# A mixture-of-experts block: three first-layer block products split once more into seven, summed in place; the first half of the slots rotated by pairs of tiles

## The chip, the cores and the metric

The kernel is one program on one core of a Trainium2 chip. The metric is the device time of one execution in microseconds (us); the figure used is the median over the runs. The engines are named as in the profile: PE (TensorE matmul; PEld its weight loads), DVE (VectorE), ACT (ScalarE), POOL (GpSimd) and SP (SyncE, which only issues DMAs here).

## The reference, cut to what matters

```
x: (4, 1024, 512) fp32, E = 8 experts, 2 per token, hidden width 2048, all fp32
z      = rotate(filter(x))               # per token, four blocks of 128 mixed by a 4x4 matrix
scores = softmax(z @ gate_w.T);  top 2 experts of each token, gates normalised
disp   = tokens sorted into 8 experts x 1024 slots
h      = relu(disp @ fc1_w.T + fc1_b)    # per expert 1024 x 512 -> 1024 x 2048
eo     = h @ fc2_w + fc2_b               # per expert 1024 x 2048 -> 1024 x 512
out    = x + sum over the two experts of gate * eo
```

The filter's gain is the same at every frequency of a channel, so filter and rotation together are one 4x4 mixing matrix M per channel.

## The kernel before, in words

A prologue of some 45 us chooses the experts, sorts the tokens into slots and gathers the first expert's rows. After it one stream runs to the end. It goes over k = 0 to 31; k is the pair (expert e, hidden group g), with four hidden groups of 512 to an expert, so e, g = divmod(k, 4).

Both layers are done by blocks with seven products in place of eight (the Winograd form of Strassen's scheme). In the first layer the blocks are halves of the hidden group, of the 512 input columns and of the 1024 slots; a product has 256 hidden rows x 256 inputs x 512 slots, two row halves m by two contraction halves c, that is four matmuls of 128x128x512. The left factors are blocks of w1 and their sums s0 to s3, made on POOL by `left1` (L131). The right factors are blocks xa, xc, xb of the rotated input and their sums x0 to x3, made on POOL once per expert (`Slots.factors`). `layer1` (L780) issues the seven products in 14 units, one per row half; a unit is what the generator does between two `yield`s. ACT (L792) or DVE (L805, L821, L832) takes each product out of PSUM, adding the bias, or another product, and the relu. The four results h11, h21, h22, r12 then give four sums of 128x1024 on DVE, s1 to s4 (`chain`, L770), the left factors of the second layer.

The second layer (`second_layers`, L959) does the same with w2: for each k two column pairs of seven products, each four matmuls of 128x128x256 (`product2`, L757), 14 units again. DVE adds each product into v tiles or the accumulators; POOL makes the sums t0 to t3 of w2.

The order is written out by hand: the last loop takes one unit of the first layer, then one of the second, in turn; the second is some three units and one k behind. After each unit `turn()` (L740) issues one piece of `background` and one of `fetches`. Background holds DVE and ACT work that has no fixed place: `chain`, the turning and rotating of the next expert's rows (`Slots.steps`, L692: 32x32 transposes of a 128x512 square, then four weighted sums, L723), and the weighted stores of finished rows (L630). Fetches are indirect DMAs of POOL: quarters of the next expert's rows (L670), choices (L611), output rows (L587). Every engine works its own list in order, and semaphores tie the lists together.

k = 0 has no sums ready and uses `layer1_plain` (L836): all eight block products, for the first 512 slots, then the second 512. Before it `rotated(0)` (L887) transposes four tiles of 128 rows on PE and forms the rotated blocks by weighted sums of 512 columns.

PSUM has eight banks of 128x512: one for `ps_x`, four for `ps_1` (two tiles of two banks), three for `ps_2`.

## Time and profile before

| what | value |
|---|---|
| time, median of 3 runs | 1624.74 us (1624.31 to 1626.83) |
| profiled execution, own time | 1616.91 us |
| its span, first to last instruction | 1615.1 us |
| mean granted PE clock | 0.990 |
| busy: PE, PEld, DVE, ACT, POOL | 1581.1, 1043.0, 910.4, 290.3, 891.6 us |
| one k in the steady part | 48.2 us |

A row of a group of instructions reads: source line, engine, operation, names written and read, shapes, count, then busy us in total and mean ns of one, then the idle time of the engine before them and who ended it. The profile records an fp32 matmul as two instructions, so a product of four matmuls is eight records. Durations of neighbouring records on PE overlap; the pace is read from the starts in the chain of waits.

### The profile page before, as it was taken

The numbers are of one execution on the slowest core, as the hardware profiler recorded it, in microseconds if no ns is written. First come the engines' busy times: TensorE is split into PE (matmuls) and PEld (weight loads), VectorE is DVE, ScalarE is ACT, GpSimd is POOL, SyncE is SP. The second block draws the span as 40 slices with busy tenths as digits, with TensorE's granted clock in tenths as the row PEclk, the third lists the DMA queues.
The fourth block names the chain that finished last, engine by engine and source line by source line (L and its number), as shares of the span: only waits on it lengthen the run. The fifth ranks groups of instructions, "written<-read, shape, count | busy, mean of one in ns | idle before, by whom it ended". The sixth has DMA issues, their size and how long they took to land.

```text
span 1615.1 us, 14666 instructions
## 1 busy us (share of the span) xinstructions
PE 1581.1 (98%) x5631; PEld 1043.0 (65%) x5631; DVE 910.4 (56%) x1292; ACT 290.3 (18%) x417; POOL 891.6 (55%) x745
## 2 busy tenths in 40 slices
PE   6899999999999999999999999999999999999997
PEld 3456666666666666666666666666666666666666
DVE  6536744476555654567455774457744576454336
ACT  3121111221112211122111221122111221111110
POOL 1676265853568445783367725586266844544305
PEclk8799999999999999999999999999999999999999
DMA  7542103311222113320133210331122311230003
GB/s 315 191 139 70 53 28 117 114 61 52 98 91 78 54 52 111 124 85 1 52 130 115 76 53 0 142 112 66 53 82 68 111 56 53 100 114 17 36 27 103
DMA packets 47998, 137.31 MB, mean 85 GB/s; under 512 B 9334, under 2 KB 9590, under 8 KB 42808
## 3 DMA queue, kind: packets, MB, share of 16 engines
q1 hardware_dynamic: 22800, 75.54, 12.8%
q0 software_dynamic: 20736, 52.32, 9.9%
q10 hardware_dynamic: 4392, 8.52, 1.4%
q8 instruction: 44, 0.72, 0.2%
q14 instruction: 26, 0.21, 0.0%
HBM read 119.77 MB, written 25.23 MB: 90 GB/s over the span
## 4 chain that ended last, share of the span: by engine, by line
PE 95%; DMA 1%; DVE 1%; POOL 1%; issue 1%; SPq 0%; POOLq 0%; ACT 0%; DVEq 0%; ACTq 0%
PE a L761 27%; PE a L748 26%; PE b L761 20%; PE b L748 20%; PE p L859 2%; DMA xb<-in_xt_dram 1%; POOL rows L587 1%; DMA rows<-in_x_dram,slot_tok 0%; POOL out_dram L635 0%; DVE A L457 0%; DMA rows<-out_dram,slot_tok 0%; PE xps L713 0%; SPq L182 0%; DVE B L444 0%; DVE xa L723 0%
## 5 line engine op out<-in xcount | busy, mean ns | idle before, releaser
L792 ACT ACTIVATE u<-a,b_sb 128x512 f32<-128x512 f32 x186 | 127.7, 686 | 793.0 <-PE a L748 793.0
L670 POOL DMA_INDIRECT xq<-in_xq_dram,quarter x224 | 232.4, 1037 | 62.0 <-issue 59.9
L761 PEld LDWEIGHTS a<-t,hs 128*128 128x128 f32 x1024 | 194.6, 190 | 79.4 <-issue 59.3
L761 PE MATMUL a<-t,hs 128*128 128x256 f32 x1024 | 241.9, 379 | 0.0
L748 PE MATMUL a<-x,s 128*128 128x512 f32 x496 | 233.1, 592 | 0.0
L136 POOL TENSOR_TENSOR s<-w 128x512 f32<-128x512 f32 x31 | 39.3, 1268 | 218.1 <-PE b L748 218.0
L139 POOL TENSOR_TENSOR s<-w,s 128x512 f32<-128x512 f32 x31 | 40.8, 1316 | 202.6 <-PE b L748 202.5
L748 PEld LDWEIGHTS a<-x,s 128*128 128x128 f32 x496 | 94.2, 190 | 65.7 <-issue 59.3
L761 PEld LDWEIGHTS b<-w,h 128*128 128x128 f32 x512 | 97.2, 190 | 42.1 <-issue 20.8
L761 PEld LDWEIGHTS a<-t,h 128*128 128x128 f32 x512 | 97.1, 190 | 40.6 <-issue 24.6
L761 PE MATMUL b<-w,h 128*128 128x256 f32 x512 | 121.1, 379 | 2.1 <-DVE acc L1051 2.1
L761 PEld LDWEIGHTS a<-w,h 128*128 128x128 f32 x512 | 97.3, 190 | 39.7 <-issue 29.7
L761 PE MATMUL a<-t,h 128*128 128x256 f32 x512 | 121.1, 379 | 0.8 <-DVE v L1025 0.8
L761 PEld LDWEIGHTS b<-t,hs 128*128 128x128 f32 x504 | 95.8, 190 | 39.5 <-issue 23.2
L761 PEld LDWEIGHTS b<-w,hs 128*128 128x128 f32 x504 | 95.8, 190 | 39.0 <-issue 27.5
L761 PE MATMUL a<-w,h 128*128 128x256 f32 x512 | 120.9, 379 | 0.0
L761 PE MATMUL b<-t,hs 128*128 128x256 f32 x504 | 119.1, 379 | 0.0
L761 PE MATMUL b<-w,hs 128*128 128x256 f32 x504 | 119.1, 379 | 0.0
L748 PE MATMUL a<-xa,w 128*128 128x512 f32 x248 | 116.6, 592 | 0.8 <-ACT u L792 0.8
L748 PE MATMUL b<-xa,w 128*128 128x512 f32 x248 | 116.5, 592 | 0.0
L748 PE MATMUL a<-x,w 128*128 128x512 f32 x248 | 116.5, 592 | 0.0
L748 PE MATMUL b<-x,s 128*128 128x512 f32 x248 | 116.5, 592 | 0.0
(183 smaller groups left out, 2158.4 us busy)
## 6 DMA issues: line engine op xcount, KB each, us to landing
w<-in_w_dram SPq DMA_DIRECT2D x64, 1024.0 KB, 7.9
xb<-in_xt_dram SPq DMA_DIRECT2D x8, 1024.0 KB, 12.2
out_dram<-in_x_dram ACTq DMA_DIRECT2D x1, 8192.0 KB
xq<-in_xq_dram,quarter POOLq DMA_INDIRECT x224, 2.5
b<-in_b_dram POOLq DMA_DIRECT2D x8, 256.0 KB, 3.7
c<-choice,slot_cho POOLq DMA_INDIRECT x64, 2.5
rows<-out_dram,slot_tok POOLq DMA_INDIRECT x64, 6.4
out_dram<-rows,slot_add POOLq DMA_INDIRECT x64, 2.8
```

What stands on the lines that cost most here:

```text
L136: lambda: G.tensor_tensor(s[0], w[:, 1, 0], w[:, 1, 1], ALU.add),
L139: lambda: G.tensor_tensor(s[3], w[:, 0, 1], s[1], ALU.subtract),
L587: nc.gpsimd.indirect_dma_start(out=t, out_offset=None, in_=src, in_offset=bass.IndirectOffsetOnAxis(ap=slot_tok[:, s : s + 1], axis=0),)
L670: nc.gpsimd.indirect_dma_start(out=self.xg[half][st][:, q * P : (q + 1) * P], out_offset=None, in_=xq, in_offset=bass.IndirectOffsetOnAxis ...
L748: nc.tensor.matmul(out[:, m], lhsT=factors[0][n][:, c, m * P : (m + 1) * P], rhs=factors[1][n][:, c, :], start=first and c == 0, stop=c == ...
L761: nc.tensor.matmul(out[m] if isinstance(out, list) else out[:, m], lhsT=factors[0][n][:, c, (st0 + m) * P : (st0 + m + 1) * P], rhs=factor ...
L792: nc.scalar.activation(to[:, m], a[:, m], func, bias=bias[:, m : m + 1])
L859: nc.tensor.matmul(ps[n][:, m], lhsT=w[:, block, i // 2, i % 2, m * P : (m + 1) * P], rhs=x.of(half, i), start=i == 0, stop=i == NJ - 1,)
```

## The change

Of the first layer's seven products, 1, 3 and 2 are done by seven products of their own blocks: 128 hidden rows x 128 inputs x 256 slots each, one matmul of 256 columns instead of a share of 512-column ones. Their left factors are made per k by `left_sub` (eight POOL sums), their right factors once per expert by `right_sub` (twelve DVE sums). Class `Within` issues them in four steps, one, two, three, four; each product goes into half of a PSUM bank, in which later products accumulate, and DVE adds the bank's state at each step straight into h11, h21 or r12 in SBUF. Products 0, 5, 6 and 4 stay whole and come first (units 0 to 7); the split ones take units 8 to 13. h tiles come from a list of eleven free tiles. `ps_x` goes to `ps_1`, now five single banks, and the squares of the next expert's rows are turned into SBUF (`sqp`) instead of PSUM. POOL's sums for the next k move from units 7, 8, 9, 13 to 9, 10, 11, 13, the second half's quarter gathers from unit 6 of g = 1 to unit 10, its turning from unit 5 of g = 2 to unit 7. `turn` issues up to two pieces of background after a unit, by the table `PACE`, and at most one where g = 0.

At the start the first half's transposes are laid out so that two tiles of rows fill two banks; the weighted sums and the products of k = 0 then go over 256 slots at a time, first the first pair.

```diff
+    def left_sub(k, w, s4):
+
+        G = nc.gpsimd
+        both = wsum.tile([P, 2, 4, P], F32, tag="sub13", name=f"sub13_{k}")
+        one = wsum.tile([P, 1, 4, P], F32, tag="sub2", name=f"sub2_{k}")
+        factors, steps = {}, []
+        for t, block, names in ((both, w[:, :, 1], (1, 3)), (one, s4.unsqueeze(1), (2,))):
+
+            def b(m, c, block=block):
+                return block[:, :, c, m * P : (m + 1) * P]
+
+            def q(i, t=t):
+                return t[:, :, i]
+
+            steps += [
+                lambda b=b, q=q: G.tensor_tensor(q(0), b(1, 0), b(1, 1), ALU.add),
+                lambda b=b, q=q: G.tensor_tensor(q(1), q(0), b(0, 0), ALU.subtract),
+                lambda b=b, q=q: G.tensor_tensor(q(2), b(0, 0), b(1, 0), ALU.subtract),
+                lambda b=b, q=q: G.tensor_tensor(q(3), b(0, 1), q(1), ALU.subtract),
+            ]
+            for n, name in enumerate(names):
+                order = (b(0, 0), b(0, 1), q(3), b(1, 1), q(0), q(1), q(2))
+                factors[name] = [f[:, n] for f in order]
+        return factors, steps
+
+    def right_sub(pool, e, right):
+
+        factors, steps = {}, []
+        for n in (1, 3, 2):
+            t = pool.tile([P, 4, HS], F32, tag=f"xsub{n}", name=f"xsub{n}_{e}")
+
+            def b(c, h, block=right[n]):
+                return block[:, c, h * HS : (h + 1) * HS]
+
+            steps += [
+                lambda b=b, t=t: V.tensor_tensor(t[:, 0], b(0, 1), b(0, 0), ALU.subtract),
+                lambda b=b, t=t: V.tensor_tensor(t[:, 1], b(1, 1), t[:, 0], ALU.subtract),
+                lambda b=b, t=t: V.tensor_tensor(t[:, 2], b(1, 1), b(0, 1), ALU.subtract),
+                lambda b=b, t=t: V.tensor_tensor(t[:, 3], b(1, 0), t[:, 1], ALU.subtract),
+            ]
+            factors[n] = [b(0, 0), b(1, 0), b(1, 1), t[:, 3], t[:, 0], t[:, 1], t[:, 2]]
+        return factors, steps
...
-    hp = ctx.enter_context(tc.tile_pool(name="hp", bufs=2))
-    up = ctx.enter_context(tc.tile_pool(name="up", bufs=2))
-    rp2 = ctx.enter_context(tc.tile_pool(name="rp2", bufs=1))
+    hp = ctx.enter_context(tc.tile_pool(name="hp", bufs=1))
+    sqp = ctx.enter_context(tc.tile_pool(name="sqp", bufs=2))
...
-    ps_x = ctx.enter_context(tc.tile_pool(name="ps_x", bufs=1, space=PSUM))
-    ps_1 = ctx.enter_context(tc.tile_pool(name="ps_1", bufs=2, space=PSUM))
+    ps_1 = ctx.enter_context(tc.tile_pool(name="ps_1", bufs=5, space=PSUM))
...
+    def bank1(name):
+        return ps_1.tile([P, HALF], F32, tag="p1", name=name)
+
+    unused = [hp.tile([P, 2, HALF], F32, name=f"hidden{i}") for i in range(11)]
...
-                bank[j] = self.bank(half, j, ps_x, "xps")
+                bank[j] = self.bank(half, j, sqp, "sq")
...
-    def turn():
-        if background:
-            background.pop(0)()
+    def turn(n=1):
+        for _ in range(n):
+            if background:
+                background.pop(0)()
...
+        if st0 + 2 == PER and 1 in tiles:
+            unused.append(factors[0][n])
...
+    class Within:
+        def __init__(self, to, left, right, name):
+            self.to, self.left, self.right = to, left, right
+            self.bank = bank1(name)
+            self.a, self.b = self.bank[:, :HS], self.bank[:, HS:]
+        def times(self, out, n, first=False):
+            nc.tensor.matmul(
+                out,
+                lhsT=self.left[n],
+                rhs=self.right[n],
+                start=first,
+                stop=True,
+                skip_group_check=True,
+            )
+        def add(self, m, h, out):
+            to = self.to[:, m, h * HS : (h + 1) * HS]
+            V.tensor_tensor(to, out, to, ALU.add)
+        def one(self):
+            self.times(self.a, 0, True)
+            self.times(self.b, 1)
+        def one_added(self):
+            self.add(0, 0, self.a)
+            self.add(0, 0, self.b)
+        def two(self, c, first):
+            self.c = c
+            self.times(self.a, 5)
+            self.times(c, 4, first)
+        def two_added(self):
+            self.add(0, 1, self.a)
+        def three(self):
+            self.times(self.a, 6)
+        def three_added(self):
+            self.add(1, 1, self.a)
+            self.add(1, 1, self.c)
+        def four(self):
+            self.times(self.a, 3)
+            self.times(self.c, 2)
+        def four_added(self):
+            self.add(1, 0, self.a)
+            self.add(0, 1, self.c)
...
+        taken = []
+        for n, bias in ((0, lo), (5, lo), (6, hi)):
+            to = unused.pop(0)
+            taken.append(to)
+            for m in range(2):
+                half(a[m], m, n, n == 0)
+                nc.scalar.activation(to[:, m], a[m], AF.Identity, bias=bias[:, m : m + 1])
+                yield
+        h11, r12, h21 = taken
+        h22 = unused.pop(0)
+        for m in range(2):
+            b = bank1(f"b{m}_{k}")
+            half(b, m, 4, True)
+            V.tensor_tensor(r12[:, m], b, r12[:, m], ALU.add)
+            V.tensor_tensor(h22[:, m], b, h21[:, m], ALU.add)
+            if m == 1:
+                relu(h22)
+            yield
+        p1, p3 = (Within(h, *(f[n] for f in subs), f"w{n}_{k}") for n, h in ((1, h11), (3, h21)))
+        p1.one()
+        p3.one()
+        p1.one_added()
+        p3.one_added()
+        yield
+        c = bank1(f"c_{k}")
+        p1.two(c[:, :HS], True)
+        p3.two(c[:, HS:], False)
+        p1.two_added()
+        p3.two_added()
+        yield
+        p1.three()
+        p3.three()
+        p2 = Within(r12, *(f[2] for f in subs), f"w2_{k}")
+        p2.one()
+        p1.three_added()
+        p3.three_added()
+        p2.one_added()
+        yield
+        p1.four()
+        p3.four()
+        p2.two(bank1(f"c2_{k}")[:, :HS], True)
+        p1.four_added()
+        relu(h11)
+        p2.two_added()
+        p3.four_added()
+        relu(h21)
+        yield
+        p2.three()
+        p2.three_added()
+        yield
+        p2.four()
+        p2.four_added()
+        s1, s2, s3, s4 = (unused.pop(0) for _ in range(4))
         hidden[k] = [h11, h21, s4, h22, s1, s2, s3]
+        chain(h11, h21, h22, s1, s2, s3, s4, r12)
+        yield
...
+        def rotated_by_pairs():
+            t = banks(0)
+            for st in range(PER):
+                for j in range(NJ):
+                    at = (j % 2 * 2 + st % 2) * P
+                    nc.tensor.transpose(
+                        t[st // 2 * 2 + j // 2][:, at : at + P],
+                        xs.xg[0][st][:, j * P : (j + 1) * P],
+                        ident,
+                    )
+            for n, slots in enumerate(PAIRS):
+                for i in range(NJ):
+                    for j in range(NJ):
+                        at = j % 2 * 2 * P
+                        xs.weighted(
+                            xs.of(0, i)[:, slots], i, j, t[n * 2 + j // 2][:, at : at + 2 * P]
+                        )
+        rotated_by_pairs()
...
+            if k:
+                subs, ahead = left_sub(k, w1_of[k], left_f[2])
+                if k == 1 or g == 0:
+                    right_subs, more = right_sub(xtp, e, xf)
+                    ahead = [f for n in range(len(ahead)) for f in (ahead[n], *more[2 * n : 2 * n + 2])]
+                    each = 3
+                else:
+                    each = 1
+                units = layer1(k, (left_f, xf), (subs, right_subs))
+            else:
+                units = layer1_plain(k, w1_next, xs)
             for i, _ in enumerate(units):
+                now[:] = k, i
+                if k and i < 8:
+                    for f in ahead[each * i : each * (i + 1)]:
+                        f()
...
-                    if (g, i) in ((0, 12 if e else 5), (1, 6)):
+                    if (g, i) in ((0, 12 if e else 5), (1, 10)):
                         fetches.extend(nxt.quarters(g))
-                    if (g, i) in ((1, 9), (2, 5)):
+                    if (g, i) in ((1, 9), (2, 7)):
                         background.extend(nxt.steps(g - 1))
...
-                if i in (7, 8, 9, 13):
+                if i in (9, 10, 11, 13):
...
+    PACE = [(1, 2)] * 6 + [(1, 1)] * 2 + [(0, 0), (0, 1), (0, 0), (0, 1), (0, 0), (0, 1)]
...
-            for gen in (first, second):
+            for n, gen in enumerate((first, second)):
                 if next(gen, "end") != "end":
                     going = True
-                turn()
+
+                k, i = now
+                pace = PACE[i][n] if 0 < k < NK - 1 else 1
+                turn(pace if k % NG else min(pace, 1))
         while background:
```

## Prediction

> **What bounds the kernel now.** I read the page first, then the chain of waits, the busy time by stage, the groups by line and form, and the timelines of the start and of one chain of sums.
>
> ```profile
> PE 1581.1 (98%) x5631; PEld 1043.0 (65%) x5631; DVE 910.4 (56%) x1292; ACT 290.3 (18%) x417; POOL 891.6 (55%) x745
> PE   6899999999999999999999999999999999999997
> PE 95%; DMA 1%; DVE 1%; POOL 1%; issue 1%; SPq 0%; POOLq 0%; ACT 0%; DVEq 0%; ACTq 0%
> ...
> 516.10 1.72 PE a L748 x4
> 517.82 1.73 PE a L761 x8
> 519.55 1.72 PE a L748 x4
> ```
>
> PE is busy throughout and makes 95% of the chain. The last three lines are the chain's pace (start, us): four records of 512 columns (two fp32 products, two records each) take 1.72 us, eight records of 256 columns the same. So a 128x128x512 product costs 0.86 us and a 256-column one 0.43: half the width is half the time.
>
> ```profile
> 467.70:515.90 48.20, 48.20 (x169) 31.91 (x169) 26.44 (x36) 9.92 (x14) 39.79 (x37) 1.00 0.30 100
> 515.90:564.10 48.20, 48.20 (x169) 31.91 (x169) 34.89 (x57) 9.92 (x14) 25.00 (x22) 1.00 0.15 51
> 564.10:612.30 48.20, 48.20 (x169) 31.91 (x169) 26.20 (x33) 7.50 (x10) 18.89 (x12) 1.00 0.13 44
> 612.30:660.50 48.20, 48.20 (x169) 31.91 (x169) 23.16 (x29) 7.61 (x10) 30.82 (x24) 1.00 0.33 117
> ```
>
> These are the four groups k = 9 to 12 (hidden groups g = 1, 2, 3, 0), with busy PE, PEld, DVE, ACT, POOL, then clock. PE has no gap at clock 1.00; DVE is at most 34.9 of 48.2 us. Only PE work is worth time here, and a wait is paid in full once PE meets it.
>
> ```profile
> L761 PEld LDWEIGHTS a<-t,hs 128*128 128x128 f32 x1024 | 194.6, 190 | 79.4 <-issue 59.3
> L1027 DVE TENSOR_TENSOR acc<-b_low,v 128x256 f32<-128x256 f32 x1 | 0.4, 414 | 0.0
> L999 DVE TENSOR_TENSOR acc<-b,v 128x512 f32<-128x512 f32 x64 | 43.9, 686 | 49.7 <-PE b L761 49.7
> L805 DVE TENSOR_TENSOR h<-b,u 128x1024 f32<-128x1024 f32 x31 | 37.7, 1217 | 12.5 <-PE b L748 12.5
> L630 DVE SCALAR_TENSOR_TENSOR rows<-acc,w,rows 128x256 f32<-128x256 f32 x6 | 2.7, 479 | 0.0
> L136 POOL TENSOR_TENSOR s<-w 128x512 f32<-128x512 f32 x31 | 39.3, 1268 | 218.1 <-PE b L748 218.0
> ```
>
> Prices (busy, mean ns). A 256-column weight load takes 190 ns against a pitch of 215, and L761 still runs without gaps.
>
> ```profile
> 518.98 1.50 POOL L139 TENSOR_TENSOR s<-w,s 128x512 f32<-128x512 f32 x1
> 519.27 2.29 DVE L774 SCALAR_TENSOR_TENSOR hs<-r,h 128x1024 f32<-128x1024 f32 x1
> L774 DVE SCALAR_TENSOR_TENSOR hs<-r,h x32: 1211/2282/2291, 88.4 to 1579.9; 128x1024 f32<-128x1024 f32 x32
> 48.83 1.97 PE L713 MATMUL xps<-ident,rows 128*128 128x128 f32 x8 [1.53 <-DMA rows<-in_x_dram,slot_tok]
> 53.49 12.07 PE L859 MATMUL p<-xa,w 128*128 128x512 f32 x24 [2.69 <-DVE xa L723]
> 87.15 1.98 PE L748 MATMUL a<-xa,w 128*128 128x512 f32 x4 [0.78 <-ACT u L792]
> ```
>
> A DVE sum of two SBUF tiles takes 1.21 us alone, 2.28 when a POOL sum runs (minimum, median). The last three lines are the start.
>
> **The change, part by part.** *PE.* Per k the first layer had 28 products of 512 columns, 28 x 0.86 = 24.1 us. Now products 0, 5, 6, 4 keep 16 (13.8 us), and 1, 3, 2 take 7 each of 256 columns (21 x 0.43 = 9.0). That is 22.8: 1.29 us less, and for 31 groups **40.0 us**. All of it lies on the path.
>
> *DVE, added.* Per k 21 in-place sums of 256 columns (0.42: 8.8 us) and four of 512 (0.69: 2.8), less three of 1024 (1.22: 3.7): +7.9, or 245 us in all. The 96 sums of right_sub read two SBUF tiles; between the PSUM sum's 0.42 and the SBUF row's 0.48 I take 0.45: 43 us. DVE goes from 910 to about 1200 of some 1575 us, 76%. In the heaviest stage it is 34.9 + 7.9 = 42.8 of 46.9 us; g = 3 gets 34 and, with the later start of its turned slots, some 3 more; g = 0 gets 23.2 + 7.9 + 5.4. It fits in every k, narrowly in g = 2. What hides these sums is PE's own 46.9 us; without it they would cost their whole length.
>
> *ACT* loses 31 instructions, gains four at the start and has 10 of 48 us: nothing.
>
> *POOL, added.* left_sub: four sums of 256 (0.67 each, L136's 1.27 over 512 columns, plus a little) and four of 128 (0.35): 4.1 us per k, 126 in all, to 1018 plus what DVE holds up. They are issued at units 0 to 7 and first needed at 9 and 11. The 16 quarter gathers moved from unit 6 to unit 10 now share POOL with sums s, t and left_sub. At 0.95 + 0.30 us apiece (the gathers in the timeline, busy and idle to the next) 16 of them take 20 us in units 0 to 7 of g = 2, with left_sub and t some 30 against 27.5. POOL ends about 3 us late; the turned slots need the gathers at unit 7, four units (14 us) after the last, landing 2.5. I price this at nothing; if the cover went, turning them would slip by the excess. SP's queue keeps order and count, POOL's DMA count stays 432.
>
> *Waits added.* In units 8 to 13 a product accumulates into a PSUM bank that DVE has just read; between lies one second-layer unit. With S8 the start of unit 8: the four products of "one" end at 0.43, 0.86, 1.29, 1.72, and "two" starts at 3.44. It must find both sums of its bank done, the second product's bank at 4.3. If DVE comes to unit 8 late by L, these are done at L + 0.84 and L + 1.68, so L may be 2.6 us. In a light k L is about 0.8 (the sums of unit 7 and one 512 sum). Unit 10 has six sums and one 512: 3.2 of 3.44 us; the tightest, c's sums, end at S8 + 10.1 against 10.75. Unit 12 is short (0.43 + 1.72): its bank must be free by S8 + 16.8, DVE has it at 16.5, or 17.2 behind a four-tile transpose (4 x 0.33). Over the six units DVE has 21 x 0.42 + 6 x 0.69 + up to 3 x 0.74 = 15.2 us of 19.4. If PE does wait, the second layer's products queue behind it, and DVE's sums behind those.
>
> *Lateness at unit 8.* The sums s1 to s4 start at unit 13 beside t0 to t2 on POOL: s2, s3, s4 at 2.0 to 2.3 each and a 0.69 need some 7 of 3.44 us, 2 to 5 us late. Unit 1 of g = 2 holds DVE for one 0.69 only (its background goes to ACT) and wins 2.8 back; units 2 to 7 need 20.0 of 20.7. So L is 2 to 3 us in the 14 groups with background, g = 2 and 3 of seven experts: the edge. The second layer bears 3.8 us (a bank is wanted 5.2 us after its product ends).
>
> *Here a rule of the Trainium skill weighs in.* Row: 2.28 against 1.21, only beside POOL sums; L630's 512-column sums take 0.74 beside indirect DMAs as without. The skill, "SBUF — State Buffer", section "SBUF: two separate sides", calls the pair of ports that DVE and GpSimd share an exclusive lock, held for a whole instruction. The turned slots move from PSUM to SBUF, so 168 weighted sums join those that need it. By the row they meet only POOL sums, 0.3 us a unit at most, included above: stalls of 0.3 us in 14 groups. By the rule read for every GpSimd instruction, each of 12 such sums in g = 2 waits half a 0.95 us gather, 6 us more: 48.8 of 46.9, 2 us over in each of the 14, 28 us. I take the row. A second rule, "PSUM — Partial Sum Buffer", section "PSUM bank collisions raise a hardware error", guards banks, not addresses; L748's 0.78 us wait on a read of the tile's other half is of that kind. By address L could be 3.0; I use 2.6.
>
> *Stalls in all:* 14 x 0.3 and a little in unit 12, **5 us**. Ends: nothing (the sums are hidden, and no wait can add time below that) and 3 us in each k, some 90; I take the near end because before, DVE worked without a gap from 563 to 583 us and PE never waited.
>
> *Start.* With pairs the 16 products on the first 256 slots need only the first two tiles' sums, of half width. All transposes still precede them on PE and end at 50.8 (48.83 + 1.97), not 53.49: 2.7 us. Three DVE sums of 0.45 a step beat PE's 1.72, so the 1.7 us lost in the 24 records (12.07 against 24 x 0.43) go; with banks as separate tiles so do 0.8 at 87.15. Sum **5 us**, between 2.7 and 6. Twelve extra DVE sums and four on ACT are inside it. What is late next is the gather of tile 2, unchanged.
>
> *Sum.* The profiled execution took 1616.91 us (span 1615.1 and 1.8 around it), 7.8 below the median of the three runs. 1616.9 - 40.0 - 5 + 5 = 1576.9, and on the median 1624.7 - 40 = **1585**.
>
> **The rivals.** *The shared port* (R1): the 28 us above with 5 from unit 12: 1624.7 - 45 + 33 = 1613. For it: medians of 2.28. Against: the 44 sums beside gathers at 0.74.
>
> *PE waits for its own sums* (R2, slower): at "two" and at unit 12, bank by bank, in every k. It decides from L = 2.6 us; break-even is 45 / 31 = 1.45 us per k. If signalling adds some 0.2 us to each of the 21 sums, DVE is 4 us later, of which 2.5 reach PE: 1624.7 + 31 x 1.05 = 1657. For it: 245 us of short dependent work, in one queue with everything else. Against: 15.2 of 19.4 us and the gapless second layer, which has the same turn between read and product.
>
> *No saving* (R3): 256-column products cost more than half. L761's pace excludes it, unless three banks in turn break the loading ahead: the same time, 1625.
>
> **How the numbers follow.** Main case 62%: 1578 (no stall, start 6.5) to 1597. R1 and stalls up to 40 us, 18%: 1597 to 1620. R3 and what balances out, 4%. R2 16%. What this measurement can tell is about 0.2%, 3.2 us: faster 0.80, same 0.04, slower 0.16. The range goes to 1619, which leaves R2, R3 and little of R1 out; the main case alone is 1578 to 1597.
>
> **What would show it.** Right: stages near 46.9 us, PE gapless, DVE 41 to 44 us in g = 2, first products near 50.8. R1: weighted sums near 1.2 us and waits only in g = 2 and 3. R2: a PE wait on the in-place sums of 1 us or more in every k. Wrong altogether: 256-column products above 0.43 us apart without a wait.

## The result: 1642.4 us, 1.1 % slower, and the profile after

| | before | after |
|---|---|---|
| median of 5 runs each | 1625.47 us (1624.31 to 1627.24) | 1642.39 us (1640.7 to 1646.35) |
| ratio | | 1.011, 95 % interval 1.0098 to 1.0122 |
| profiled execution, own time; span | 1616.91; 1615.1 us | 1646.35; 1644.6 us |
| mean granted PE clock | 0.990 | 0.979 |
| start of k = 1 to start of k = 31 | 1443.8 us | 1473.9 us |

The forecast was 1585 us, and faster; the change is 17 us slower. The two profiled executions are 29.4 us apart, the medians 16.9: after's ran 4.0 us over its median, and before's, at 1616.91, lies under all five of its timed runs. By the profiles, on which the stage times below rest, the change costs 29.4 us.

In the new numbering the first layer's whole products are L894 (were L748), the second layer's L805 (L761), the split products L839, their in-place sums L850, the transposes of the next expert's rows L736 (L685), the weighted sums L776 (L723), the quarter gathers L721 (L670), the weighting of finished rows L681 (L630) and their stores L686 (L635). The page, its rows of PE and the chain:

```profile
PE 1564.1 (95%) x6221; PEld 1163.7 (71%) x6221; DVE 1201.3 (73%) x2082; ACT 285.5 (17%) x390; POOL 1113.5 (68%) x993
PE   5899999899998999989999899989999899999997
...
PE 59%; DVE 17%; POOL 15%; issue 5%; DMA 3%; SPq 0%; POOLq 0%; DVEq 0%
```

PE fell from 98% to 95% of a longer span. Before, its row was nines throughout; now there is an 8 every four or five slices, that is once per expert (a slice is 41 us, an expert takes 4.8 of them). The chain was PE for 95%; now DVE has 17% of it and POOL 15%. DVE is at the 1200 us forecast. Something takes the saving back once per expert. The four groups k = 12 to 15 (g = 0, 1, 2, 3), then one stretch inside the second; columns are length, busy PE, PEld, DVE, ACT, POOL, the granted clock, DMA share and GB/s:

```profile
622.10:671.20 49.10, 47.21 (x187) 35.19 (x186) 36.45 (x60) 7.30 (x9) 31.26 (x29) 1.00 0.31 102
671.20:724.90 53.70, 49.23 (x188) 36.44 (x188) 32.96 (x53) 7.91 (x10) 46.62 (x45) 0.97 0.29 96
724.90:773.00 48.10, 47.25 (x188) 35.26 (x187) 41.31 (x71) 10.46 (x14) 38.31 (x35) 1.00 0.18 58
773.00:819.90 46.90, 46.90 (x187) 35.29 (x186) 38.10 (x67) 8.53 (x11) 27.00 (x20) 1.00 0.13 46
...
713.10:717.70 4.60, 3.92 (x10) 2.93 (x11) 3.16 (x8) 0.00 (x0) 4.14 (x4) 0.65 0.13 33
```

Every group took 48.2 us before. The last, g = 3, has no gap and is at 46.9, the forecast value. g = 2 loses 1.1 us, g = 0 some 2.2, and g = 1 loses 6.7. DVE is not the engine that is full there (33.0 of 53.7 us); POOL is, with 46.6. From the starts of the groups in the trace, over k = 4 to 30 (27 groups), the time above 46.97 us a group is 41.9 us in g = 1 (six of its seven groups), 18.5 in g = 0 and 6.7 in g = 2: **67 us of stalls** against 27 x 1.24 = 33.5 us saved. The three groups before those save another 3.6, which makes the +30 us of the table. The waits:

```profile
POOL out_dram L686 <- DVE rows L681: 106.0, 18, 9.1
POOL out_dram L635 <- DVE rows L630: 34.4, 19, 5.2
...
DVE xps L736 <- DMA xq<-in_xq_dram,quarter: 32.9, 6, 5.9
...
PE w L839 <- DVE hidden L850: 30.2, 13, 4.5
...
PE b L805 <- DVE acc L1214: 15.7, 8, 2.4
```

The columns are us in total, times, longest; the second line is before's, the others after's. PE waits for the in-place sums (L850), up to 4.5 us; DVE waits six times for a gathered quarter of the next expert's rows, 5.5 us each, always in a g = 1; POOL waits for the weighted rows. Before, PE waited nowhere in the steady part, DVE never for a gathered quarter, and POOL 34.4 us for the rows. How they hang together, in the group of k = 13, is read from POOL's and then from DVE's timeline (start, duration, and in brackets the idle time before and its cause):

```profile
660.68 1.02 POOL L686 DMA_INDIRECT out_dram<-rows,slot_add  x1 [9.08 <-DVE rows L681]
668.32 1.01 POOL L686 DMA_INDIRECT out_dram<-rows,slot_add  x1 [4.09 <-DVE rows L681]
...
709.84 0.95 POOL L721 DMA_INDIRECT xq<-in_xq_dram,quarter  x1 [0.30 <-issue]
```
```profile
705.89 0.69 DVE L1217 TENSOR_TENSOR acc<-b,v 128x512 f32<-128x512 f32 x1 [1.73 <-PE b L805]
706.50 0.69 DVE L736 STREAM_TRANSPOSE xps<-xq 128x128 f32<-128x128 f32 x3
712.46 0.31 DVE L736 STREAM_TRANSPOSE xps<-xq 128x128 f32<-128x128 f32 x1 [5.28 <-DMA xq<-in_xq_dram,quarter]
712.70 0.38 DVE L850 TENSOR_TENSOR hidden<-w,hidden 128x256 f32<-128x256 f32 x1
```

In g = 0 POOL stands idle for 9.1 and 4.1 us in front of two row stores whose rows DVE has not weighted yet. Behind them in POOL's list are the other stores and the 16 gathers of the next expert's first half. The last of those gathers is issued at 709.84. DVE has transposed three tiles, and its next instruction is the transpose of the fourth: it idles 5.28 us until that quarter lands. The in-place sum that PE waits for (L850) stands behind the transpose in DVE's list, and so PE stops for 4.0 us. After the gap the granted clock is at half: the window 713.10 to 717.70 above shows 0.65 on average. In the trace the half lasts 3.4 us, which costs 1.7 more, and nearly all of g = 1's 6.7 is told: 4.0, 1.7, and about 1 in two smaller waits around it.

### The profile page after: what moved, and what is told of

Read it like the earlier page. It is cut to its first block, busy times and chain, and to the rows that moved or that the text cites. A ratio compares the mean times of both kernels' runs of the same rounds, so it can differ in the third digit from the quotient of the medians.

```text
span 1644.6 us, 17016 instructions
## 1 busy us (share of the span) xinstructions
PE 1564.1 (95%) x6221; PEld 1163.7 (71%) x6221; DVE 1201.3 (73%) x2082; ACT 285.5 (17%) x390; POOL 1113.5 (68%) x993
## 4 chain that ended last, share of the span: by engine, by line
PE 59%; DVE 17%; POOL 15%; issue 5%; DMA 3%; SPq 0%; POOLq 0%; DVEq 0%
PE a L805 16%; PE b L805 13%; PE w L839 10%; PE a L894 9%; POOL xq L721 7%; PE c L839 5%; PE b L894 4%; DVE xa L776 3%; POOL out_dram L686 3%; PE p L981 2%; DVE hidden L821 2%; DVE hidden L820 2%; DVE hidden L819 1%; DMA xb<-in_xt_dram 1%; DVE xps L736 1%
## 5 line engine op out<-in xcount | busy, mean ns | idle before, releaser
L805 PE MATMUL a<-t,hidden 128*128 128x256 f32 x1536 | 364.2, 380 | 0.8 <-DVE v L1188 0.8
L805 PEld LDWEIGHTS a<-t,hidden 128*128 128x128 f32 x1536 | 293.0, 191 | 80.9 <-issue 38.8
L721 POOL DMA_INDIRECT xq<-in_xq_dram,quarter x224 | 246.4, 1100 | 52.3 <-issue 48.3
L805 PE MATMUL b<-w,hidden 128*128 128x256 f32 x1016 | 243.6, 383 | 15.7 <-DVE acc L1214 15.7
L805 PEld LDWEIGHTS b<-w,hidden 128*128 128x128 f32 x1016 | 193.8, 191 | 71.3 <-issue 22.2
L894 PE MATMUL a<-x,s 128*128 128x512 f32 x496 | 234.9, 596 | 0.0
L909 ACT ACTIVATE hidden<-a,b_sb 128x512 f32<-128x512 f32 x186 | 127.8, 687 | 606.1 <-PE a L894 564.7
L850 DVE TENSOR_TENSOR hidden<-w,hidden 128x256 f32<-128x256 f32 x465 | 190.5, 419 | 45.2 <-PE w L839 37.0
L827 ACT ACTIVATE hidden<-hidden 128x1024 f32<-128x1024 f32 x93 | 98.3, 1057 | 640.8 <-DVE hidden L850 390.4
L686 POOL DMA_INDIRECT out_dram<-rows,slot_add x64 | 66.5, 1039 | 117.6 <-DVE rows L681 106.0
L894 PEld LDWEIGHTS a<-x,s 128*128 128x128 f32 x496 | 95.3, 192 | 67.3 <-issue 60.7
L805 PEld LDWEIGHTS a<-w,hidden 128*128 128x128 f32 x512 | 97.3, 190 | 39.7 <-issue 29.7
L805 PE MATMUL a<-w,hidden 128*128 128x256 f32 x512 | 120.9, 379 | 0.0
L805 PE MATMUL b<-t,hidden 128*128 128x256 f32 x504 | 119.1, 379 | 0.0
L894 PE MATMUL b<-x,s 128*128 128x512 f32 x248 | 116.5, 592 | 0.0
L894 PE MATMUL a<-xa,w 128*128 128x512 f32 x248 | 116.4, 592 | 0.0
L805 PEld LDWEIGHTS b<-t,hidden 128*128 128x128 f32 x504 | 95.8, 190 | 26.2 <-issue 11.5
L839 PE MATMUL w<-xsub,sub 128*128 128x256 f32 x372 | 107.9, 386 | 6.0 <-DVE hidden L850 6.0
L850 DVE TENSOR_TENSOR hidden<-c,hidden 128x256 f32<-128x256 f32 x186 | 78.6, 423 | 26.8 <-PE c L839 23.4
```

The source lines that it names most:

```text
L686: nc.gpsimd.indirect_dma_start(out=out_of[st], out_offset=bass.IndirectOffsetOnAxis(ap=slot_add[:, s : s + 1], axis=0), in_=self.rows[st], ...
L721: nc.gpsimd.indirect_dma_start(out=self.xg[half][st][:, q * P : (q + 1) * P], out_offset=None, in_=xq, in_offset=bass.IndirectOffsetOnAxis ...
L805: nc.tensor.matmul(out[m] if isinstance(out, list) else out[:, m], lhsT=factors[0][n][:, c, (st0 + m) * P : (st0 + m + 1) * P], rhs=factor ...
L827: nc.scalar.activation(h, h, AF.Relu)
L839: nc.tensor.matmul(out, lhsT=self.left[n], rhs=self.right[n], start=first, stop=True, skip_group_check=True,)
L850: V.tensor_tensor(to, out, to, ALU.add)
```

## The experiments

The theory after this first reading: (a) g = 1 is a late gather, made late by POOL's order and by the weighted rows; (b) g = 0 is DVE's own lateness, the twelve `right_sub` sums meeting POOL's sums beside s1 to s4; (c) g = 2 is the weighted sums of squares that now lie in SBUF. The rival for all three is R2 of the prediction: 245 us of short sums are too much for DVE, and it is late wherever one looks. Runs were made on more than one chip (the kernel before took 1617.8 us on one, 1624.5 and 1625.1 on others), so each ratio is taken to the kernel before on the run's own chip, and for the causes I compare the stretch from k = 1 to k = 31 of the profiles; 46.97 us is a group without a stall. Losses are sums over k = 4 to 30. In g = 1 to 3 they stand in six groups, since the last expert has no next one; in g = 0 in seven. A loss "a group" below is the mean over these.

| kernel | k = 1 to 31, us | lost in g = 0, 1, 2, 3, us | median, us | ratio to before (95 %) |
|---|---|---|---|---|
| before | 1443.8 | (no gap, 48.21 each) | 1625.47 | |
| after | 1473.9 | 18.5, 41.9, 6.7, 0 | 1642.39 | 1.011 (1.0098 to 1.0122) |
| e1, turning two units later | 1430.0 | 15.2, 0.5, 0, 6.8 | 1600.42 | 0.9896 (0.9879 to 0.9912) |
| e2, rows weighted earlier | 1440.6 | 23.9, 6.8, 3.1, 0 | 1610.83 | 0.9966 (0.9952 to 0.998) |
| e3, right_sub two units later | 1454.3 | 0, 40.8, 6.7, 0 | 1624.62 | 1.0049 (1.0032 to 1.0066) |
| e4, squares in PSUM | 1467.8 | 18.5, 40.0, 3.1, 0 | 1641.13 | 1.0146 (1.0129 to 1.0163) |
| e5, e1 with e3 | 1414.8 | 0, 0.5, 0, 6.8 | 1586.74 | 0.9765 (0.9752 to 0.9778) |
| e6, e1 with e3 and e4 | 1410.7 | 0, 3.7, 0.6, 0 | 1580.71 | 0.9733 (0.9719 to 0.9746) |
| e7, left_sub once | 1429.1 | 4.0, 19.4, 0, 0 | 1601.54 | 0.9862 (0.9847 to 0.9877) |
| e9, e6 with the turning at unit 13 | 1412.6 | 0, 0, 4.9, 0 | 1584.57 | 0.9748 (0.9735 to 0.9761) |

**e1: the transposes of the first half start at unit 11 instead of unit 9.**

```diff
-                    if (g, i) in ((1, 9), (2, 7)):
+                    if (g, i) in ((1, 11), (2, 7)):
```

> The changed kernel, with the turning of the next expert's first half started after unit 11 of g = 1 instead of unit 9; nothing else. Theory (gather): the 6.7 us that each g = 1 loses are DVE standing in its order before a transpose whose gathered rows have not landed, and PE behind it, first waiting, then at half clock. Two units later the rows are there: g = 1 takes about 47 us instead of 53.7, six times 6.7, so about 1600 us instead of 1642. Rival (in-place sums): PE waits since DVE has too much work around units 8 to 13, wherever the transposes stand: the time stays at 1635 to 1645.

Measured: 1600.42 us, ratio 0.9896. Its windows for the same four groups:

```profile
605.10:654.20 49.10, 47.20 (x188) 35.17 (x187) 36.46 (x60) 7.29 (x9) 31.23 (x29) 1.00 0.31 102
654.20:701.30 47.10, 47.10 (x188) 35.23 (x187) 32.91 (x53) 7.30 (x9) 41.30 (x40) 1.00 0.31 104
701.30:748.20 46.90, 46.90 (x187) 35.30 (x186) 39.25 (x71) 10.36 (x14) 41.03 (x40) 1.00 0.22 65
748.20:796.30 48.10, 47.24 (x187) 35.26 (x186) 39.75 (x67) 9.13 (x12) 27.37 (x20) 1.00 0.12 44
```

g = 1 fell from 53.7 to 47.1 and has the full clock. No sum was taken from DVE, and the gathers are as late as in after (the sixteenth is issued 38.5 us into g = 1); only the place of the transposes moved, by 6.9 us, and DVE waits for no quarter any more. So it was the wait for the gather, not the amount of DVE's work, and the rival falls for g = 1. The 1.1 us of g = 2 moved to g = 3, with the weighted sums that the turning pushes ahead of it.

**e2: one piece of background after each unit in g = 0.** There `PACE` gives 19 chances in a g = 0, where the kernel before had 28.

```diff
-                turn(pace if k % NG else min(pace, 1))
+                turn(pace if k % NG else 1)
```

> The changed kernel, with one piece of background after every unit where g = 0, as before the change, also in units 8 to 13 (the table allows three there). Theory (stores): the gathers are late because POOL stands about 13 us in g = 0 before two row stores whose weighting DVE has not been given yet; with the weighting issued at once POOL's queue moves on, the last gather lands some 8 us earlier and the stall of g = 1 goes: 1600 to 1625 us, less what eight weighted sums of 0.74 us cost between the in-place sums of g = 0. Rival (POOL's new sums): POOL is late because of left_sub's 4 us per k; then the stall stays, 1632 to 1645.

Measured: 1610.83 us, ratio 0.9966. POOL's stores at the end of g = 0:

```profile
645.51 1.01 POOL L686 DMA_INDIRECT out_dram<-rows,slot_add  x1 [9.07 <-DVE rows L681]
648.67 1.00 POOL L686 DMA_INDIRECT out_dram<-rows,slot_add  x1 [0.84 <-DVE rows L681]
649.98 0.97 POOL L686 DMA_INDIRECT out_dram<-rows,slot_add  x1 [0.30 <-DVE rows L681]
653.10 0.99 POOL L686 DMA_INDIRECT out_dram<-rows,slot_add  x1 [0.84 <-DVE rows L681]
```

Four stores lie in front of g = 1 (which starts at 656.6), as in the kernel before; in after it was two, with six left for g = 1. g = 1 loses 1.1 us a group. It isn't free: g = 0 went from 18.5 to 23.9 us. Of these 5.4 us, 3.7 are a second wait of 0.5 us a group for the in-place sums, near the end of g = 0, where the pieces now come; 1.7 are one more stretch at half clock.

**e7: the eight sums of left_sub are made for k = 1 only,** and the same tiles are used for the other 30 groups, whose sums are left out.

```diff
+        if k == 1:
+            kept.append(wsum.tile([P, 2, 4, P], F32, tag="sub13", name=f"sub13_{k}"))
+            kept.append(wsum.tile([P, 1, 4, P], F32, tag="sub2", name=f"sub2_{k}"))
+        both, one = kept
...
-        return factors, steps
+        return factors, steps if k == 1 else [lambda: None] * 8
```

> The changed kernel, with POOL's eight sums of left_sub made for k = 1 only; later groups use those stale tiles, so 30 x 4.1 us of POOL's work are left out and everything else stays. If POOL's added sums help to make the gathers late, the last gather of the first half lands 4 to 6 us earlier in g = 1 and most of its 6.7 us stall goes: about 1600 to 1612 us on a chip where the kernel before takes 1618. If the late row stores alone do it, the stall stays: 1628 to 1636.

Measured: 1601.54 us, ratio 0.9862. g = 1 loses 3.2 us a group instead of 7.0, g = 0 loses 0.6 instead of 2.6, g = 2 nothing. With e2 this makes a series for g = 1; the gather is the sixteenth of the next expert's first half, in the group of k = 13, taken from POOL's timelines:

| | row stores in g = 0, then in g = 1 | sixteenth gather issued, after the start of g = 1 | DVE's waits for a quarter, whole run | the group's loss |
|---|---|---|---|---|
| before | 4, 4 | 28.7 us | none | none |
| e2 | 4, 4 | 34.6 us | 5, 7.4 us | 1.0 us |
| e7 | 2, 6 | 35.4 us | 1, 1.5 us | 4.2 us |
| after | 2, 6 | 38.6 us | 6, 32.9 us | 6.7 us |

The gather came 9.9 us later in after than before: e2 takes back 4.0 of it by the stores, e7 3.2 by left_sub's sums; the rest these two runs don't tell. So the lateness has two causes on one queue.

e7's loss in g = 1 is not the gather's alone. It is a wait of PE of 2.0, some smaller ones and 1.7 for half the clock, and in front of the transposes DVE stood still for something else:

```profile
687.77 0.69 DVE L1220 TENSOR_TENSOR acc<-b,v 128x512 f32<-128x512 f32 x1 [3.85 <-PE b L808]
688.38 0.88 DVE L739 STREAM_TRANSPOSE xps<-xq 128x128 f32<-128x128 f32 x4
```

This is L1217 of after's fence above. There it starts 34.65 us into g = 1, in all seven groups, as soon as PE has finished the product that it reads. In e7 PE finishes that product at the same time, but DVE starts at 36.3 to 38.2 us in the six groups with gathers, and at 34.65 in the seventh, which has none: PE's semaphore reaches it up to 3.6 us late. Had L1220 started at 34.65, the fourth transpose would still have had to wait until some 37.9 us (an estimate: 35.4 and the 2.5 us from issue to landing of before's page). So part of e7's loss would remain, how much is not shown. What delays the semaphore is open; e8 has the same.

**e3: right_sub's sums two units later,** at units 2 to 7 in place of 0 to 5, so that s2 to s4 are done first.

```diff
-                    ahead = [f for n in range(len(ahead)) for f in (ahead[n], *more[2 * n : 2 * n + 2])]
-                    each = 3
+                    at = max(0, 2)
+                    each = [[f] for f in ahead] + [[]] * 6
+                    for n in range(6):
+                        each[n + at] = each[n + at] + more[2 * n : 2 * n + 2]
...
-                    for f in ahead[each * i : each * (i + 1)]:
+                    for f in each[i]:
```

> The changed kernel, with the twelve sums of right_sub moved two units later (units 2 to 7 instead of 0 to 5) in k = 1 and where g = 0; POOL's left_sub stays. Theory (lock): g = 0 loses 2.2 to 3.9 us at unit 3 because s1 to s4, four sums of right_sub and POOL's sums take turns at the shared port in units 13 to 1, so that the sum that frees a second-layer bank comes late; apart from each other the stall goes: 49.1 becomes 47 us, some 15 us in all, about 1627. Rival (the chain s1 to s4 alone is too late): g = 0 stays at 49 or more, 1640 to 1645.

Measured: 1624.62 us, ratio 1.0049. First DVE's timeline in after at the start of a g = 0:

```profile
624.85 0.94 DVE L182 TENSOR_TENSOR xsub<-xa 128x256 f32<-128x256 f32 x1
625.82 1.37 DVE L183 TENSOR_TENSOR xsub<-xa,xsub 128x256 f32<-128x256 f32 x1
627.12 2.29 DVE L819 TENSOR_TENSOR hidden<-hidden,hidden 128x1024 f32<-128x1024 f32 x1
...
633.27 2.28 DVE L821 TENSOR_TENSOR hidden<-hidden,hidden 128x1024 f32<-128x1024 f32 x1
635.48 0.68 DVE L1214 TENSOR_TENSOR acc<-a,acc 128x512 f32<-128x512 f32 x1
```

then in e3:

```profile
617.88 2.29 DVE L821 TENSOR_TENSOR hidden<-hidden,hidden 128x1024 f32<-128x1024 f32 x1
620.09 0.68 DVE L1216 TENSOR_TENSOR acc<-a,acc 128x512 f32<-128x512 f32 x1
```

In after two `right_sub` sums of 256 columns take 0.94 and 1.37 us (0.41 and 0.42 in groups where no POOL sum runs beside them), and so does everything around them. The sum that frees a second-layer bank (L1214) starts at 635.48, 13.4 us into the group; in e3 the same sum (L1216) starts at 620.09, 8.8 us into it. Of PE's 15.7 us of waits on L1214 only one of 2.4 us is left, after k = 31 has begun, and g = 0 runs at 46.97 us in all seven groups. That it is the meeting with POOL and not DVE's work alone is shown by e7: with `right_sub` in its old place and only left_sub's sums gone, g = 0 loses 0.6 us a group. (b) holds.

**e4: the squares go to a PSUM bank of their own again,** with four banks left for the first layer.

```diff
-    sqp = ctx.enter_context(tc.tile_pool(name="sqp", bufs=2))
+    ps_x = ctx.enter_context(tc.tile_pool(name="ps_x", bufs=1, space=PSUM))
...
-    ps_1 = ctx.enter_context(tc.tile_pool(name="ps_1", bufs=5, space=PSUM))
+    ps_1 = ctx.enter_context(tc.tile_pool(name="ps_1", bufs=4, space=PSUM))
...
-                bank[j] = self.bank(half, j, sqp, "sq")
+                bank[j] = self.bank(half, j, ps_x, "xps")
...
-            return [xs.bank(half, j, *((ps_1, "p1") if j == 3 else (ps_2, "p2"))) for j in range(NJ)]
+            return [xs.bank(half, j, *((ps_x, "xps") if j == 3 else (ps_2, "p2"))) for j in range(NJ)]
```

> The changed kernel, with the turned squares back in a PSUM bank of their own, and four banks for the first layer instead of five. Theory (lock): the 168 weighted sums then have one SBUF input and no longer take turns with POOL (0.74 us each instead of 1.0 to 1.4 beside POOL's sums); g = 2 loses its 1.1 us stall: 48.1 becomes 47.0, some 8 us, about 1634; g = 1 keeps its stall. Rival (banks): the fifth bank was needed, a product in unit 11 waits for a bank that DVE is still reading: 0.3 to 1 us more in every k, 1650 to 1670.

Measured: 1641.13 us, ratio 1.0146. The weighted sums by source line (minimum/median/maximum ns, first and last start), in after and in e4:

```profile
L776 DVE SCALAR_TENSOR_TENSOR xa<-xps,M,xa x108: 472/742/2176, 48.7 to 1347.9; 128x512 f32<-128x512 f32 x84, 128x256 f32<-128x256 f32 x24
```
```profile
L776 DVE SCALAR_TENSOR_TENSOR xa<-xps,M,xa x108: 473/741/752, 47.3 to 1340.7; 128x512 f32<-128x512 f32 x84, 128x256 f32<-128x256 f32 x24
```

From PSUM a weighted sum never takes more than 0.752 us, from SBUF up to 2.176. (c) holds for half of g = 2, whose loss falls from 1.1 to 0.5 us a group; that e7 clears g = 2 altogether says that POOL's new sums have part in it. The whole is no better: in the profile e4 gains 6 us from k = 1 to k = 31, while its ratio is above after's. Since after was not run on e4's chip, what of the ratio belongs to the chip stays open.

**e5 and e6: the moves together.** e5 is e1 with e3, e6 is e5 with e4.

> The changed kernel with both moves: the turning two units later (g = 1) and right_sub two units later (g = 0). If the two stalls are separate and the sums' place is all, what each move gave alone adds up: the group times become 46.97 us for g = 0, 1 and 2 and 48.1 for g = 3, 15 us below the late turning alone (ratio 0.990 to the kernel before), so a ratio of 0.980 to 0.982. Rival (one wait takes the place of the other: DVE's work in g = 0 and 1 is what binds, not where it stands): less than 8 us of the 15 come, a ratio of 0.985 or more.

> As the kernel with both moves, and the turned squares back in a PSUM bank of their own with four first-layer banks. With the squares in SBUF g = 3 still loses 1.1 us, in one weighted sum that stands 2.2 us before POOL's sum of the right blocks. With one SBUF input that wait is gone: g = 3 at 46.97 to 47.4 us, 3 to 7 us less than the kernel with both moves, ratio 0.976 to 0.979. Rival (the bank given up costs a wait in the short units): no better or slower than with both moves.

Measured on one chip: 1586.74 us (0.9765) and 1580.71 us (0.9733, 95 % 0.9719 to 0.9746). The page of e6, and its windows for g = 0, 1, 2:

```profile
PE 1544.5 (98%) x6221; PEld 1155.8 (73%) x6221; DVE 1182.7 (75%) x2082; ACT 282.8 (18%) x390; POOL 1072.9 (68%) x993
```
```profile
596.80:643.70 46.90, 46.90 (x187) 35.30 (x186) 35.64 (x60) 7.29 (x9) 31.55 (x29) 1.00 0.32 107
643.70:691.30 47.60, 47.35 (x187) 35.26 (x187) 33.33 (x53) 7.30 (x9) 41.83 (x40) 1.00 0.30 103
691.30:738.40 47.10, 47.10 (x188) 35.30 (x187) 38.77 (x71) 10.19 (x14) 38.76 (x40) 1.00 0.20 65
```

PE is at 98% again, with every product, sum and gather of the change in place. All that R2 blamed, the 651 in-place sums with DVE at 75%, is still there, and the groups lose 4.3 us by them in all. e6 is the fastest kernel of the study, 43.8 us under the kernel before on this chip. The stage times tell less: from span to span of the profiles it is 35.5 us (1615.1 to 1579.6). The other 8 are the 1624.5 us that the kernel before takes here against 1616.9 in its profile. The same holds for e5, whose ratio came out under the forecast 0.980: its 15.2 us from e1 to e5 are the forecast's 15.

**e9: e6 with the turning at unit 13.** e6's g = 1 still loses 0.6 us a group, of this sort on DVE:

```profile
686.77 1.40 DVE L736 STREAM_TRANSPOSE xps<-xq 128x128 f32<-128x128 f32 x4
688.08 0.40 DVE L850 TENSOR_TENSOR hidden<-w,hidden 128x256 f32<-128x256 f32 x1
```

Four transposes into PSUM stand before the in-place sum that unit 12 needs; PE starts 0.41 us late.

> As the kernel with both moves and squares in PSUM, with the first half's turning started after unit 13 of g = 1 instead of unit 11. There g = 1 still loses 0.5 us: the four transposes (1.40 us into PSUM) stand between the second-layer sum and the sums that free unit 12's bank. Moved behind unit 13 they stand before no in-place sum: g = 1 at 46.97 us, 3 to 4 us less, ratio 0.971 to 0.973. Rival: the transposes that are missing in units 11 to 13 come too late in g = 2, which then loses 0.5 us or more at its own unit 8 to 10, and nothing is won: 0.973 to 0.975.

Measured: 1584.57 us, ratio 0.9748 (0.9735 to 0.9761). g = 1 is clean, and g = 2 loses 0.8 us a group: the same four transposes met the same unit there. Moved, not removed; e6's place is as good.

**e8: the start by pairs alone,** on the kernel before.

```diff
+    PAIRS = (slice(0, 2 * P), slice(2 * P, 4 * P))
...
-            for i in range(NJ):
+            parts = PAIRS if half == 0 else (slice(0, HALF),)
+            for at, i in ((at, i) for at in parts for i in range(NJ)):
...
-                            rhs=x.of(half, i),
-                            start=i == 0,
+                            rhs=x.of(half, i)[:, at],
+                            start=i == 0 and at.start == 0,
...
-        rotated(0)
+        rotated_by_pairs()
```

> The kernel before with the start of the change alone: transposes, weighted sums and products of the first 512 slots by pairs of tiles; PSUM banks as before. As predicted, 5 us less (ratio 0.997). If the 1.7 us of the first 24 records were the clock, which is at half until 56 us in both profiles, and not the sums, only the earlier first product remains: 2.5 to 3.5 us, ratio 0.998. Rival: nothing, since the gathers set the start.

Measured: 1622.51 us, ratio 0.9987 (0.998 to 0.9994): 2 us, not 5. k = 1 starts at 82.2 us in its profile, at 84.5 in before's. The same profile also loses 1.05 us in six of the seven g = 1 groups, which before's doesn't; PE waits there for ACT, and ACT starts late. In the group of k = 13, which starts at 660.40 in e8 and at 660.56 in before, first e8's lines, then before's:

```profile
691.39 1.88 PE L750 MATMUL a<-x,s 128*128 128x512 f32 x4
694.60 0.69 ACT L794 ACTIVATE u<-a,b_sb 128x512 f32<-128x512 f32 x1 [3.98 <-PE a L750]
```
```profile
691.55 1.88 PE L748 MATMUL a<-x,s 128*128 128x512 f32 x4
693.47 0.69 ACT L792 ACTIVATE u<-a,b_sb 128x512 f32<-128x512 f32 x1 [2.70 <-PE a L748]
```

PE makes the product 31.0 us into the group in both. ACT reads it at 32.9 us in before, at 34.1 to 34.2 in e8, in the six groups with gathers; in the seventh, without them, at 32.9 in both. So it is the late semaphore of e7 again. Those 6.3 us, in groups that are built like before's, are close to the 7 us by which the chips differ for the kernel before, and to the 8.6 by which its profiled execution ran under its median. No profile of before on that chip exists, so that this is the same wait is a guess.

## Why the prediction was wrong, step by step

**Right: the saving on PE.** A group without a stall is 46.97 us against 48.21, 1.24 of the 1.29 us forecast, so products of half the width do take half the time. R3 is excluded.

**Right: the in-place sums and their waits.** 0.42 us a sum was the price, and it holds:

```profile
L850 DVE TENSOR_TENSOR hidden<-w,hidden 128x256 f32<-128x256 f32 x465 | 190.5, 419 | 45.2 <-PE w L839 37.0
```

DVE came out at 1201 us of a forecast 1200. The allowance L of 2.6 us at unit 8 was enough in g = 3, and with the moves of e6 nearly everywhere. The 0.4 us that I counted in unit 12 behind a four-tile transpose is the 0.41 of e6. The stop where R2 put it, PE waiting on L850, did appear, but not from R2's cause: the sums were not slow or too many. They stood behind an instruction that waited for a DMA.

**Wrong: "POOL, added", and this decides.** I wrote that POOL ends about 3 us late and "I price this at nothing; if the cover went, turning them would slip by the excess". Two things failed in it. I looked at the gathers that the change moved, those of the second half, in g = 2, and there they did no harm: DVE waits for none of them. I did not look at the first half's gathers, which the change leaves in place and which share POOL with the new left_sub sums and with the row stores in g = 1. Nor did I ask what `PACE` does in g = 0: with 19 pieces of background instead of 28 the rows are weighted later, the stores wait for the rows, and everything in POOL's list waits for the stores. The term put at 0 measured 41.9 us. (POOL's busy time came to 1113.5 us, 95 above the 1018 to which the forecast added "what DVE holds up" without a number; what these 95 are made of is not shown.) And a slip does not push a late transpose back by its excess alone: DVE works in order, so the excess goes to whatever stands behind it, here the sum that PE needs next. The prediction asked of each added wait what is queued behind it on DVE, but this wait it did not see.

**Wrong: the price of right_sub and "Lateness at unit 8".** I took 0.45 us for each of its sums, between the prices of a PSUM sum and of an undisturbed SBUF sum. But they read two SBUF tiles, and the row that I had quoted myself (2.28 against 1.21 us beside a POOL sum) applied to them. Four of them took 0.94, 1.37, 0.94 and 0.94 in g = 0, 4.2 us in place of 1.8, in the very units where s1 to s4 meet POOL. I had set the edge in g = 2 and 3 and looked for it at unit 8; it came in g = 0, at the second-layer bank for which I had allowed 3.8 us (L1214, 4.6 us later than in e3). The term was near 0; it measured 18.5 us.

**Wrong by size: the weighted sums from SBUF.** 14 x 0.3 us forecast; 6.7 us measured, and g = 2 only: 1.1 in six groups. The choice of row over rule stands: the Trainium skill ("SBUF — State Buffer", "SBUF: two separate sides") names an exclusive lock between DVE and GpSimd, and read for every GpSimd instruction it gave 28 us in g = 2 and 3. The page itself narrows it: a DVE instruction with two SBUF inputs needs the lock only against a GpSimd instruction that reads SBUF. The trace has the long weighted sums only beside POOL sums; the 42 that met gathers alone stay at 0.73 to 0.75 us.

**Half the clock** was in no term. From k = 1 to k = 31 eight stretches at half clock, 30.7 us together, cost some 15 of the 67 us.

**Wrong by size: the start.** 5 us forecast, 2 measured (e8). The 1.7 us "lost in the 24 records" were not DVE's: the granted clock in the trace is at half until some 56 us in both kernels, and the first four of those records, before that time, ran at half speed, which is 1.6 us. Nor is L748's 0.78 us wait at 87.15 an instance of the PSUM rule beside which I put it: the half that ACT reads and the half that PE writes next are two banks of one tile, so it is a wait by tile.

With the two stalls moved away most of the sum is there. That e6 is 43.8 us under the kernel before, and the sum without stalls was 45, is in part luck: by the profiles the gain is 35.5, and the rest is the time by which the kernel before runs over its own profile.

## What to carry to other kernels

Ask of every in-order queue what stands in it in each stage, and follow the work that the change did not touch but that shares the queue: here the loss came from gathers whose code is the same before and after, behind stores that waited for sums that a new table made late. An instruction that may wait for a DMA should not stand in front of one that the bound engine needs within a few us; two units of distance, one number in the code, turned 1.1 % slower into 1.0 % faster. When a change that should pay loses, find which stages lose and by how much before calling the whole idea too dear: three stages had three causes, two of them removed by moving work by two units. And compare kernels by stage where one program differs by 7 us from chip to chip.

## What the runs showed of the hardware

- A wait of PE can cost more than its length. In after's trace each of the six gaps of 3.8 to 4.5 us was followed by 3.4 us or more at half clock; gaps of 1.9 us did so in two of seven cases, gaps up to 0.9 us never. The Trainium skill ("TensorE: Matmul & The Clock Gate", "Part 1: The HAM clock gate") gives an idle window of about 3.4 us for the drop. The 4 us gaps agree; the 1.9 us gaps, and e7's of 2.0 us (0.83 granted over the 10 us around it), show that a shorter wait can also be enough.
- Which of the 1.9 us gaps do so depends on where they fall. Within each run, all changes of the granted clock lie on a grid of 3.41 us. After, e1, e2 and e4 have 28 such gaps, all at the same place of g = 0. The 7 that began 0.2 to 1.1 us after a point of the grid brought half clock, the 21 that began 1.5 to 3.1 us after one did not.
- A semaphore of PE can come late. In e7 and e8 DVE or ACT started 0.8 to 3.6 us later than in a run where PE finished the same product at the same time, seen only in g = 1 and only while the next expert's rows are gathered. Before, after, e1 to e6 and e9 gather as well and show none of it, so the gathers alone do not make it; the cause is open.
- DVE sums with two SBUF inputs can lose time beside POOL sums, not beside POOL's indirect DMAs: in after 0.73 to 0.75 us beside gathers, up to 2.44 beside POOL's sums for the same 512 columns. Alternating sums on both engines then pace each other: 128x1024 sums of 1.21 us alone took 2.28.
- DVE transposes of 128x128 took 0.27 us apiece into SBUF and 0.33 into PSUM (four in a row, overlapping into SBUF, in 0.88 and 1.40 us); the squares of e4 are of the second kind.
